# Far sets of a fused square-root and spectral kernel: turned tiles as moving operands only, the second one sent through memory

## The chip, the cores and the metric

The kernel runs on one core of one Trainium2 chip. The metric is device time in microseconds (us) of one launch. A core has five engines with their own instruction queues, each in order: TensorE (PE in the profile; its weight loads are PEld), VectorE (DVE), ScalarE (ACT), GpSimd (POOL) and SyncE (SP), which here only issues DMA transfers. ScalarE issues DMA transfers too. Matmuls write to PSUM, which has 8 banks; an instruction waits for others by semaphores.

## The reference

Two residual layers on x of shape (32, 32, 128, 128). The first normalises x by groups of channels and adds to x an approximate matrix square root of each of its 1024 matrices of 128 x 128, found by five coupled Newton-Schulz steps. The second normalises again and adds a spectral convolution.

```python
normA = sqrt(sum(A2 * A2, axis=(1, 2)))
Y, Z = A2 / normA, I
for _ in range(5):
    T = 0.5 * (3.0 * I - Z @ Y)
    Y, Z = Y @ T, T @ Z
x = x + Y * sqrt(normA)                      # of the group-normalised x
...
f = fftn(group_norm(x), axes=(2, 3)).real    # 32 x 32 corner modes, top and bottom
x = x + ifftn(einsum over channels(f, weights)).real
```

## The kernel before, in words

Four channels of one image make a set; there are 32 x 8 = 256 sets. A set is one generator, `newton` (line 447), which does a few products, yields, and goes on a round later. Up to eight sets are under way in eight lanes; a round goes through the lanes in order and lets each do one step. Line 88 keeps every instruction in program order on its engine, so the order of each queue is the order in which the rounds reach the steps. A new set starts every 23/8 rounds while far sets come (`FAR`, line 42). Far sets are those of images 1 to 18 (`is_far`, line 357): 144 sets. The others are near sets.

A set's work is a polynomial of m, the scaled matrix, put as products of four 128 x 128 matrices (`products`, line 345: four float32 matmuls, stationary operand first, into one PSUM bank). Each far set needs products with a transposed tile, and gets it without TensorE: VectorE turns each 32 x 32 block of a PSUM bank into the tile "turn" (0.7 us), and DMA transfers move the blocks to their places. `across` (line 420) does both: one transposition and four transfers on SP, one for each quarter of the partitions.

In this document step k is what a far set does after its k-th yield. Before the change:

- step 0: product of mb and m; the bank is turned and goes by four transfers into w; VectorE adds v to the same bank; GpSimd forms EYE_Q minus mb in place
- step 4: product of v and w; VectorE makes q
- step 6: product of q and m; ScalarE writes y, the first half of the tile "my"
- step 8: product of q and y; ScalarE writes the new m, the second half of "my"; then the bank is turned and goes by four transfers into mb, in runs of 32 numbers (128 bytes)
- step 10: GpSimd forms v = EYE_V minus m
- step 12: product of mb and m, in the profile "ps<-my,mb"; as step 0, with the transfers into w
- step 16: product of v and w; q
- step 18: four matmuls of double width, q times y and m side by side; ScalarE writes t and y4
- step 20: product of t and q; VectorE makes t
- step 22: product of t and y4, added to x

In the names of the profile the moving operand comes first: "ps<-my,mb" has mb stationary. Near sets use other steps, with transpositions on TensorE, and their own "my,mb", with mb copied by ScalarE.

Around the sets, in the same rounds, GpSimd and ScalarE scale the next sets' inputs (`staged`, line 374; x is m and b is mb of step 0); ScalarE issues the loads of coming inputs (`fetch`, line 366, and `prep`, line 222); SP stores each finished set into the scratch tensor mid (`settle`, line 496). `four` (line 312) hands out the buffers of each kind; `rooms` (lines 308 and 309) has two numbers for each: those that stay, and those there until the far sets are done.

Of the kernel before, what the change touches and what calls it, by code (L numbers as in the profile page):

```python
# [93 lines left out]
def conv_preact_kernel(  # L94
# [19 lines left out]
    nc.vector.tensor_scalar_mul(eye1[:, 0, :], ident, EYE)  # L114
    eye = eye1.to_broadcast([P, 4, P])
    eyes = []
    for n, f in (("v", EYE_V), ("q", EYE_Q), ("p", EYE_Q * TURNED)):
        e = const.tile([P, 1, P], F32, name=f"eye_{n}")
        nc.vector.tensor_scalar_mul(e[:, 0, :], ident, f)
        eyes.append(e.to_broadcast([P, 4, P]))  # L120
# [101 lines left out]
    def prep(bs, made):  # L222

        n = len(bs)
        nc_, ng = n * C, n * G
        first_b = bs[0]
        st = small.tile([P, ng, 6], F32, tag="a_st", name=f"a_st{first_b}", bufs=2)
        tiles = []
        parts = [(b, i) for b in bs for i in range(C // 4)]

        ahead = 3 if first_b else 8

        def load(k):
            b, i = parts[k]
            if first_b or i < 4:
                t = stp.tile([P, 2, 2 * P], F32, tag="xs", name=f"xs{b}_{i}")
            else:
                t = four("turn", True).rearrange("p (j c) x -> p j (c x)", j=2)
            src = xs_in[b, :, 2 * i : 2 * i + 2].rearrange("p g h c -> p g (h c)")
            kept(nc.scalar.dma_start(out=t, in_=src))  # L240
            tiles.append(t)

        for k in range(ahead):
            load(k)
        yield
        for k in range(len(parts)):
            for j in range(2):
                nc.vector.bn_stats(st[:, 2 * k + j, :], tiles[k][:, j, :])
            yield
            if k + ahead < len(parts):  # L250
                load(k + ahead)
        ms = small.tile([P, ng], F32, tag="a_ms", name=f"a_ms{first_b}")
        nm, d = yield from moments(st, ms, "a")
        yield from pause
        pq = bank()[:, 0, 0:nc_]
        nc.tensor.matmul(pq, avg_mean, d.rearrange("p g c -> p (g c)"), start=True, stop=True)
        if not first_b:
            warm(5)

        v = small.tile([P, nc_ + ng], F32, tag="a_v", name=f"a_v{first_b}")  # L260
        nc.vector.tensor_scalar_mul(v[:, 0:nc_], pq, -512 / (P * P))
        yield
        vg = small.tile([P, ng], F32, tag="a_vg", name=f"a_vg{first_b}")
        nc.vector.tensor_reduce(
            vg, v[:, 0:nc_].rearrange("p (g c) -> p g c", c=2), AX.X, ALU.add
        )
        nc.vector.tensor_scalar(v[:, nc_:], vg, 0.5, EPS, ALU.mult, ALU.add)
        yield
        s = small.tile([P, nc_ + ng], F32, tag="a_r_s", name=f"a_r_s{first_b}", bufs=2)
        yield from root(v, nc_ + ng, s)  # L270
        iv = small.tile([P, nc_ + ng], F32, tag="a_inv", name=f"a_inv{first_b}")
        nc.vector.reciprocal(iv, s)
        yield

        sc = small.tile([P, nc_], F32, tag="a_sc", name=f"a_sc{first_b}", bufs=2)
        nc.vector.tensor_scalar_mul(sc, iv[:, 0:nc_], MS / P)
        off = small.tile([P, ng, 2], F32, tag="a_off", name=f"a_off{first_b}", bufs=2)
        nc.vector.tensor_tensor(
            off,
            sc.rearrange("p (g c) -> p g c", c=2),  # L280
            nm[:, :, None].to_broadcast([P, ng, 2]),
            ALU.mult,
        )
        off = off.rearrange("p g c -> p (g c)")
        sn = small.tile([P, nc_], F32, tag="a_t_s", name=f"a_t_s{first_b}", bufs=3)
        for k, b in enumerate(bs):
            g, c = slice(k * G, k * G + G), slice(k * C, k * C + C)
            made[b] = (nm[:, g], sc[:, c], off[:, c], sn[:, c])
        yield
        nn = small.tile([P, ng, 2], F32, tag="a_d", name=f"a_n{first_b}")  # L290
        nc.vector.tensor_tensor(
            nn,
            s[:, 0:nc_].rearrange("p (g c) -> p g c", c=2),
            iv[:, nc_:, None].to_broadcast([P, ng, 2]),
            ALU.mult,
        )
        nn = nn.rearrange("p g c -> p (g c)")
        for far in sorted({is_far(b) for b in bs}):
            of = [k for k, b in enumerate(bs) if is_far(b) == far]
            c = slice(of[0] * C, of[-1] * C + C)  # L300
            f = EYE_Q * QS * TURNED**2 if far else EYE * QF
            nc.vector.tensor_scalar_mul(nn[:, c], nn[:, c], P * (1.5 / f) ** 2)
        yield
        yield from root(nn, nc_, sn)
        yield


    rooms = dict(b=(4, 4), xt=(10, 4), x=(3, 2), r=(4, 0), v=(3, 4), w=(3, 2), q=(4, 2))
    rooms.update(my=(4, 2), mb=(2, 3), t=(3, 2), y4=(2, 2), turn=(0, 4))
    turns = dict.fromkeys(rooms, 0)  # L310

    def four(tag, more):
# [22 lines left out]
    def blocks(t):  # L335


        return t.rearrange("p c x -> p (c x)").rearrange("p (a c j) -> p a c j", a=4, c=4)

    def minus(eye, m, t):  # L340

        nc.gpsimd.tensor_tensor(t, eye, m, ALU.subtract)
        return t
# [13 lines left out]
    def is_far(b):  # L357
        return 0 < b < FIRST
# [15 lines left out]
    def staged(b, g, nm, sc, off, sn):  # L374
# [10 lines left out]
        for j in range(4):  # L385
# [13 lines left out]
                on_scalar(m[:, j, :], xt[:, j, :], off, sc, c)  # L399
            on_scalar(mb[:, j, :], mb[:, j, :], off, sc, c)  # L400
            yield
        v = minus(eye_v, m, four("v", True)) if is_far(b) else None
        ready.append((xt, m, mb, v))
        yield

# [11 lines left out]
        yield from rest  # L417
        return q

    def across(ps, more, into):  # L420


        t = four("turn", more)
        nc.vector.transpose(blocks(t), ps.rearrange("p c (i b) -> p b c i", b=4))
        for a in range(4):
            src = t[32 * a : 32 * a + 32].rearrange("p c x -> p (c x)")
            kept(
                nc.sync.dma_start(out=into(a), in_=src.rearrange("p (b x) -> p b x", b=4))
            )

    def far_quartic(m, mb, v, more, f, eye_q):

        ps = products(mb, m)
        w = four("w", more)
        across(ps, more, lambda a: w.rearrange("p c x -> p (c x)")[:, P * a : P * a + P])
        nc.vector.scalar_tensor_tensor(v, ps, 1 / (9 * MS * f), v, ALU.mult, ALU.add)
        minus(eye_q, mb, mb)
        yield from rest
        yield from rest
        ps = products(v, blocks(w).rearrange("p a c j -> p c a j"))  # L440
        q = plus(ps, 9 / (39 * MS**2), mb, "q", more)
        yield from rest
        return q

# [2 lines left out]
    def newton(g, sn, xt, m, mb, v, far, more):  # L447


        qf = QS if far else QF  # L450
        if far:
            q = yield from far_quartic(m, mb, v, more, 1.0, eye_q)
        else:
            q = yield from near_quartic(m, mb, more)
        my = four("my", more)
        y = my[:, :, 0, :]
        nc.scalar.mul(y, products(q, m), 1 / (MS * qf))
        yield from rest
        m = my[:, :, 1, :]
        ps = products(q, y)  # L460
        nc.scalar.mul(m, ps, MS / qf)
        if far:
            mb = four("mb", more)
            across(ps, more, lambda a: mb[:, :, 32 * a : 32 * a + 32])
            yield from rest
            v = minus(eye_v, m, four("v", more))
            yield from rest
            qf, et, eye_t = QS * TURNED, EYE_Q * TURNED, eye_p
            q = yield from far_quartic(m, mb, v, more, TURNED, eye_p)
        else:  # L470
            yield from rest
            mb = taken(transposed(m), "mb", more)
            yield from rest
            et, eye_t = EYE, eye
            q = yield from near_quartic(m, mb, more)
        both = [bank().rearrange("p (j k) x -> p j k x", k=2) for _ in range(2)]
        for j in range(4):
            nc.tensor.matmul(both[j // 2][:, j % 2], q[:, j], my[:, j], start=True, stop=True)
        w, y = four("t", more), four("y4", more)
        for h in range(2):  # L480
            nc.scalar.mul(w[:, 2 * h : 2 * h + 2, :], both[h][:, :, 1, :], 1 / (MS * qf))
        for j in range(4):
            c = 4 * g + j
            nc.scalar.mul(y[:, j, :], both[j // 2][:, j % 2, 0, :], sn[:, c : c + 1])
        yield from rest
        t = plus(products(w, q), -0.5 * et / (1.5 * qf), eye_t, "t", more)
        yield from rest
        nc.vector.tensor_tensor(xt, products(t, y), xt, ALU.add)
        if not todo and lanes.count(None) == LANES - 1:
            warm(2)  # L490
        yield
# [707 lines left out]
```

## Time and profile before

| what | us |
|---|---|
| median of 3 runs | 3038.55 |
| lowest and highest | 3033.91, 3040.33 |
| the profiled execution, its own time | 3030.63 |
| its span, first to last instruction | 3028.5 |
| TensorE busy in the span | 2856.4 (94%) |
| VectorE busy | 2271.7 (75%) |
| GpSimd busy | 1995.5 (66%) |
| ScalarE busy | 1567.5 (52%) |

The durations below come from that one profiled execution. Matmul records overlap, so the starts of successive products tell TensorE's pace better than their durations. The chain of waits that ended last has 51% of the span on TensorE's matmuls, 17% on DMA transfers (4% w, 3% mb) and 5% on SP's queue. DMA moved 598.69 MB in 746612 packets, 403472 of them under 512 bytes.

### The profile page before, as it was taken

Reading aid. Unit: us, or ns where it says so; the run is one execution under the profiler, and the core shown is the slowest. Engines: PE = TensorE matmul, PEld = TensorE weight load, DVE = VectorE, ACT = ScalarE, POOL = GpSimd, SP = SyncE. Lnnn points to the kernel's source line nnn. Section 1 sums busy time; section 2 is a strip of 40 time slices with the busy share of each in tenths; the row PEclk is TensorE's granted clock in tenths of the full one; section 3 lists DMA queues with packets and bytes.
Section 4 is the critical chain, followed back from the end, with each engine's and each line's share of the span. In section 5 each row is a group of like instructions: output and inputs, shape, how many; then the busy total and the mean of one; then the engine's idle time right before and its main releaser. Section 6 shows DMA issues by size and latency. Waiting matters only on the chain.

```text
span 3028.5 us, 73234 instructions
## 1 busy us (share of the span) xinstructions
PE 2856.4 (94%) x26536; PEld 2636.7 (87%) x26536; DVE 2271.7 (75%) x4407; ACT 1567.5 (52%) x4043; POOL 1995.5 (66%) x2308
## 2 busy tenths in 40 slices
PE   7999999999999999999999999999989999999996
PEld 7999988989989898898899889888878899888884
DVE  7878787878878787878776645877886867777564
ACT  4555555555545555555544445555554544555452
POOL 4677766777767676777665534787777754678352
PEclk9999999999999999999999999999999999999997
DMA  5577777778676877777753566877867747666676
GB/s 178 153 202 173 197 181 178 185 181 205 165 199 166 210 167 204 171 204 174 199 137 99 160 208 206 269 245 252 274 231 253 246 123 214 214 220 216 179 223 247
DMA packets 746612, 598.69 MB, mean 198 GB/s; under 512 B 403472, under 2 KB 564240, under 8 KB 746256
## 3 DMA queue, kind: packets, MB, share of 16 engines
q1 hardware_dynamic: 632640, 385.56, 46.9%
q10 hardware_dynamic: 113616, 208.45, 21.7%
q8 instruction: 215, 3.52, 0.5%
q14 instruction: 141, 1.16, 0.1%
HBM read 326.93 MB, written 153.62 MB: 159 GB/s over the span
## 4 chain that ended last, share of the span: by engine, by line
PE 51%; DMA 17%; DVE 10%; POOL 9%; issue 5%; SPq 5%; ACT 2%; ACTq 1%; DVEq 0%; POOLq 0%
PE ps L88 51%; SPq L88 5%; DMA w<-turn 4%; DMA mb<-turn 3%; POOL yt L88 3%; DMA yt<-mid 2%; DMA mid<-xt 2%; POOL r L88 2%; POOL fold L88 2%; DVE turn L88 2%; POOL x L88 2%; DMA xs<-in_xs 1%; DVE v L88 1%; DVE yt L88 1%; DVE q L88 1%
## 5 line engine op out<-in xcount | busy, mean ns | idle before, releaser
L88 PE MATMUL ps<-my,q 128*128 128x128 f32 (+1 forms) x4096 | 749.7, 331 | 41.3 <-ACT my L88 21.0
L88 PEld LDWEIGHTS ps<-my,q 128*128 128x128 f32 x4096 | 623.6, 192 | 94.7 <-ACT my L88 23.6
L88 ACT ACTIVATE b<-b,a_off,a_sc 128x128 f32<-128x128 f32 x1024 | 467.9, 491 | 348.3 <-DMA b<-in_x 63.8
L88 PE MATMUL ps<-w,v 128*128 128x128 f32 x4096 | 550.4, 279 | 40.5 <-DVE w L88 15.9
L88 PEld LDWEIGHTS ps<-w,v 128*128 128x128 f32 x4096 | 499.7, 193 | 56.6 <-issue 23.4
L88 POOL TENSOR_TENSOR fold<-xt 128x256 f32<-128x256 f32 x512 | 363.7, 733 | 247.1 <-DVE xt L88 220.6
L88 ACT ACTIVATE my<-ps 128x512 f32<-128x512 f32 x512 | 305.7, 599 | 413.9 <-PE ps L88 386.3
L88 POOL TENSOR_TENSOR yt<-yt,d 128x512 f32<-128x512 f32 x244 | 306.8, 1282 | 221.5 <-ACT d L88 190.5
L88 DVE STREAM_TRANSPOSE turn<-ps 128x512 f32<-128x512 f32 x432 | 302.8, 705 | 178.4 <-ACT my L88 102.1
L88 POOL TENSOR_TENSOR v<-eye_v,x 128x512 f32<-128x512 f32 x144 | 183.6, 1275 | 262.7 <-ACT x L88 255.7
L88 POOL TENSOR_SCALAR x<-xt,a_nm,a_sc 128x128 f32<-128x128 f32 x736 | 324.9, 457 | 15.1 <-DVE a_sc L88 14.8
L88 ACT ACTIVATE t<-ps 128x256 f32<-128x256 f32 x512 | 186.9, 380 | 268.9 <-PE ps L88 255.6
L88 ACT ACTIVATE y<-ps,a_t_s 128x128 f32<-128x128 f32 x1024 | 291.4, 375 | 0.0
L88 PE MATMUL ps<-my,mb 128*128 128x128 f32 x2048 | 275.5, 278 | 10.7 <-DMA mb<-turn 4.8
L88 PE MATMUL ps<-x,b 128*128 128x128 f32 x2048 | 281.3, 280 | 1.1 <-ACT b L88 1.0
L88 PE MATMUL ps<-x,q 128*128 128x128 f32 x2048 | 277.5, 279 | 4.6 <-DVE q L88 2.6
L88 PE MATMUL ps<-q,t 128*128 128x128 f32 x2048 | 275.0, 278 | 6.8 <-ACT t L88 6.2
L88 PEld LDWEIGHTS ps<-my,mb 128*128 128x128 f32 x2048 | 259.8, 193 | 22.1 <-issue 9.1
L88 PE MATMUL ps<-y,t 128*128 128x128 f32 x2048 | 275.0, 278 | 0.3 <-DVE b_r L88 0.3
L88 POOL TENSOR_TENSOR mb<-eye_p,mb 128x512 f32<-128x512 f32 x144 | 184.0, 1278 | 133.1 <-PE ps L88 130.9
L88 PEld LDWEIGHTS ps<-x,q 128*128 128x128 f32 x2048 | 252.2, 194 | 15.9 <-issue 8.4
L88 PEld LDWEIGHTS ps<-q,t 128*128 128x128 f32 x2048 | 251.1, 193 | 9.2 <-ACT t L88 7.3
(132 smaller groups left out, 4776.4 us busy)
## 6 DMA issues: line engine op xcount, KB each, us to landing
w<-turn SPq DMA_DIRECT2D x1152, 64.0 KB
b<-in_x ACTq DMA_DIRECT2D x256, 256.0 KB
xt<-in_xt ACTq DMA_DIRECT2D x256, 256.0 KB
mid<-xt SPq DMA_DIRECT2D x256, 256.0 KB
yt<-mid SPq DMA_DIRECT2D x128, 512.0 KB
xs<-in_xs ACTq DMA_DIRECT2D x252, 256.0 KB
out<-yt SPq DMA_DIRECT2D x115, 512.0 KB
mb<-turn SPq DMA_DIRECT2D x576, 64.0 KB
```

The lines of the kernel that those rows point to most:

```text
L88: return self.tc.keep_in_program_order(issue(*args, **kw))
```

## The change

In far sets the other factor of each product becomes the stationary one, so that a turned tile is only ever the moving operand, which can be read in blocks. The second m's tile may then land in the block order in which w lands, in runs of 512 bytes. Its way is no longer four transfers from "turn" to mb in step 8, but one transfer from "turn" to a scratch tensor in memory in step 8, and one from there to mb in step 10. With this:

- in step 8 the transposition stands ahead of ScalarE's copy of the same bank
- v of the second quartic is formed in step 12 from mb as it landed, instead of in step 10 from m; VectorE adds to it in step 13 instead of step 12 (`later`)
- the subtraction in place is done on m, not on mb
- step 18 is two products of single width: q times mb, which ScalarE copies at once, and q times y
- b and mb have one more early buffer each
- constants are scaled for the tile that is used

```diff
-    for n, f in (("v", EYE_V), ("q", EYE_Q), ("p", EYE_Q * TURNED)):
+    for n, f in (("v", EYE_V), ("q", EYE_Q), ("p", EYE_V * TURNED)):
...
-    rooms = dict(b=(4, 4), xt=(10, 4), x=(3, 2), r=(4, 0), v=(3, 4), w=(3, 2), q=(4, 2))
-    rooms.update(my=(4, 2), mb=(2, 3), t=(3, 2), y4=(2, 2), turn=(0, 4))
+    rooms = dict(b=(4, 5), xt=(10, 4), x=(3, 2), r=(4, 0), v=(3, 4), w=(3, 2), q=(4, 2))
+    rooms.update(my=(4, 2), mb=(2, 4), t=(3, 2), y4=(2, 2), turn=(0, 4))
...
+    def turned(ps, more):
         t = four("turn", more)
         nc.vector.transpose(blocks(t), ps.rearrange("p c (i b) -> p b c i", b=4))
+        return t
+
+    def by_rows(t):
+        return blocks(t).rearrange("p a c j -> p c a j")
+
+    def far_quartic(m, mb, v, f, later, more):
+        ps = products(m, mb)
+        t, w = turned(ps, more), four("w", more)
         for a in range(4):
             src = t[32 * a : 32 * a + 32].rearrange("p c x -> p (c x)")
...
-        nc.vector.scalar_tensor_tensor(v, ps, 1 / (9 * MS * f), v, ALU.mult, ALU.add)
-        minus(eye_q, mb, mb)
-        yield from rest
+        minus(eye_q, m, m)
+        if later:
+            yield
+        nc.vector.scalar_tensor_tensor(v, ps, 1 / (9 * MS), v, ALU.mult, ALU.add)
+        if not later:
+            yield
+        yield
         yield from rest
-        ps = products(v, blocks(w).rearrange("p a c j -> p c a j"))
-        q = plus(ps, 9 / (39 * MS**2), mb, "q", more)
+        q = plus(products(v, by_rows(w)), 9 / (39 * MS**2 * f**2), m, "q", more)
...
-        ps = products(q, y)
-        nc.scalar.mul(m, ps, MS / qf)
+        ps = products(y, q) if far else products(q, y)
         if far:
+            t = turned(ps, more)
+            held = dram.tile([P, 512], F32, name="turn", tag="turn", bufs=4)
+            kept(nc.sync.dma_start(out=held, in_=t.rearrange("p c x -> p (c x)")))
+            nc.scalar.mul(m, ps, MS / qf)
+            yield from rest
             mb = four("mb", more)
-            across(ps, more, lambda a: mb[:, :, 32 * a : 32 * a + 32])
+            src = held.rearrange("(a i) (b x) -> (i b) a x", a=4, b=4)
+            into = mb.rearrange("p c x -> p (c x)").rearrange("p (a x) -> p a x", a=4)
+            kept(nc.sync.dma_start(out=into, in_=src))
             yield from rest
-            v = minus(eye_v, m, four("v", more))
-            yield from rest
-            qf, et, eye_t = QS * TURNED, EYE_Q * TURNED, eye_p
-            q = yield from far_quartic(m, mb, v, more, TURNED, eye_p)
+            v = four("v", more)
+            form = "p c (a j) -> p c a j"
+            minus(eye_p.rearrange(form, a=4), by_rows(mb), v.rearrange(form, a=4))
+            q = yield from far_quartic(m, by_rows(mb), v, TURNED, True, more)
+            w, y4 = four("t", more), four("y4", more)
+            nc.scalar.mul(w, products(q, by_rows(mb)), 1 / (MS * qf * TURNED))
+            ps = products(q, y)
+            for j in range(4):
+                c = 4 * g + j
+                nc.scalar.mul(y4[:, j, :], ps[:, j, :], sn[:, c : c + 1])
```

`rest` is two yields, so the steps keep their numbers.

More of the change, by code (lines that the diff above doesn't have):

```diff
@@ L300, in prep @@
             c = slice(of[0] * C, of[-1] * C + C)
-            f = EYE_Q * QS * TURNED**2 if far else EYE * QF
+            f = EYE_Q * QS if far else EYE * QF
             nc.vector.tensor_scalar_mul(nn[:, c], nn[:, c], P * (1.5 / f) ** 2)
@@ L401, in staged @@
             yield
-        v = minus(eye_v, m, four("v", True)) if is_far(b) else None
+        v = minus(eye_v, mb, four("v", True)) if is_far(b) else None
         ready.append((xt, m, mb, v))
@@ L418, in near_quartic @@
         return q
-    def across(ps, more, into):
+    def turned(ps, more):
         t = four("turn", more)
         nc.vector.transpose(blocks(t), ps.rearrange("p c (i b) -> p b c i", b=4))
+        return t
[4 more added lines that the diff above has]
+        t, w = turned(ps, more), four("w", more)
         for a in range(4):
@@ L427, in across @@
             kept(
-                nc.sync.dma_start(out=into(a), in_=src.rearrange("p (b x) -> p b x", b=4))
-            )
[L431 to L435, printed above, removed]
-        nc.vector.scalar_tensor_tensor(v, ps, 1 / (9 * MS * f), v, ALU.mult, ALU.add)
-        minus(eye_q, mb, mb)
+                nc.sync.dma_start(
+                    out=w.rearrange("p c x -> p (c x)")[:, P * a : P * a + P],
+                    in_=src.rearrange("p (b x) -> p b x", b=4),
+                )
+            )
+        minus(eye_q, m, m)
[5 more added lines that the diff above has]
+        yield
         yield from rest
-        yield from rest
-        ps = products(v, blocks(w).rearrange("p a c j -> p c a j"))
-        q = plus(ps, 9 / (39 * MS**2), mb, "q", more)
+        q = plus(products(v, by_rows(w)), 9 / (39 * MS**2 * f**2), m, "q", more)
         yield from rest
@@ L447, in newton @@
     def newton(g, sn, xt, m, mb, v, far, more):
-        qf = QS if far else QF
+        qf, et, eye_t = (QS, EYE_Q, eye_q) if far else (QF, EYE, eye)
         if far:
-            q = yield from far_quartic(m, mb, v, more, 1.0, eye_q)
+            q = yield from far_quartic(m, mb, v, 1.0, False, more)
         else:
@@ L456, in newton @@
         y = my[:, :, 0, :]
-        nc.scalar.mul(y, products(q, m), 1 / (MS * qf))
+        nc.scalar.mul(y, products(q, mb if far else m), 1 / (MS * qf))
         yield from rest
         m = my[:, :, 1, :]
-        ps = products(q, y)
-        nc.scalar.mul(m, ps, MS / qf)
+        ps = products(y, q) if far else products(q, y)
         if far:
+            t = turned(ps, more)
[3 more added lines that the diff above has]
+            yield from rest
             mb = four("mb", more)
-            across(ps, more, lambda a: mb[:, :, 32 * a : 32 * a + 32])
+            src = held.rearrange("(a i) (b x) -> (i b) a x", a=4, b=4)
+            into = mb.rearrange("p c x -> p (c x)").rearrange("p (a x) -> p a x", a=4)
+            kept(nc.sync.dma_start(out=into, in_=src))
             yield from rest
-            v = minus(eye_v, m, four("v", more))
-            yield from rest
-            qf, et, eye_t = QS * TURNED, EYE_Q * TURNED, eye_p
-            q = yield from far_quartic(m, mb, v, more, TURNED, eye_p)
+            v = four("v", more)
[8 more added lines that the diff above has]
+                nc.scalar.mul(y4[:, j, :], ps[:, j, :], sn[:, c : c + 1])
         else:
+            nc.scalar.mul(m, ps, MS / qf)
             yield from rest
@@ L473, in newton @@
             yield from rest
-            et, eye_t = EYE, eye
             q = yield from near_quartic(m, mb, more)
[L476 to L484, printed above, removed]
+            both = [bank().rearrange("p (j k) x -> p j k x", k=2) for _ in range(2)]
+            for j in range(4):
+                nc.tensor.matmul(both[j // 2][:, j % 2], q[:, j], my[:, j], start=True, stop=True)
+            w, y4 = four("t", more), four("y4", more)
+            for h in range(2):
+                nc.scalar.mul(w[:, 2 * h : 2 * h + 2, :], both[h][:, :, 1, :], 1 / (MS * qf))
+            for j in range(4):
+                c = 4 * g + j
+                nc.scalar.mul(y4[:, j, :], both[j // 2][:, j % 2, 0, :], sn[:, c : c + 1])
         yield from rest
@@ L487, in newton @@
         yield from rest
-        nc.vector.tensor_tensor(xt, products(t, y), xt, ALU.add)
+        ps = products(y4, t) if far else products(t, y4)
+        nc.vector.tensor_tensor(xt, ps, xt, ALU.add)
         if not todo and lanes.count(None) == LANES - 1:
```

## The prediction

> **What bounds the kernel now.** I read the shares by engine first, then the stage by windows. The transfers of turned tiles, which only far sets have, run from 89.4 to 1570.2 us (below), so the stretch from 90 to 1575 us counts. The windows view gives it one line (length, then busy us and instructions of PE, PEld, DVE, ACT and POOL, granted clock, DMA share, GB/s):
>
> ```profile
> 90.00:1575.00 1485.00, 1416.70 (x11589) 1333.61 (x11588) 1204.92 (x2390) 800.37 (x2127) 1058.15 (x1170) 0.99 0.74 184
> ```
>
> The reader is to see that TensorE is idle for only 1485.0 − 1416.7 = 68 us here, 0.47 us a set: the stage's 1163 double-width matmul records, eight a set, make 145 sets of 10.2 us (the 144 far ones and a near neighbour). That is all a better hidden transfer can win. VectorE is busy for 81%, so it often runs behind. The waits view of the stage says what the idle time hung on (total, times, longest), first for PE, then for DVE:
>
> ```profile
> PE ps L88 <- ACT my L88: 17.2, 8, 3.7
> PE ps L88 <- DMA mb<-turn: 11.9, 10, 3.5
> PE ps L88 <- DVE q L88: 10.0, 11, 1.3
> ```
>
> ```profile
> DVE turn L88 <- ACT my L88: 102.1, 91, 4.5
> DVE turn L88 <- PE ps L88: 65.9, 91, 1.4
> ```
>
> So the trip of the second m costs TensorE 12 us today, and VectorE loses 102 us because the transposition of step 8 stands behind ScalarE's copy of the same bank. Next the issuing engine: the view of tile "turn" has issue times in ns (min/median/max), the timeline of SP shows them in a row, and the timeline of PE the same stretch:
>
> ```profile
> L88 SPq DMA_DIRECT2D w<-turn x1152: 542/602/1930, 89.4 to 1570.2; - x192
> L88 SPq DMA_DIRECT2D mb<-turn x576: 609/632/1985, 110.2 to 1558.2; - x192
> ```
>
> ```profile
> 743.91 2.83 SPq L88 DMA_DIRECT2D mb<-turn  x4
> 746.79 0.62 SPq L88 DMA_DIRECT2D mid<-xt  x1
> 747.51 5.13 SPq L88 DMA_DIRECT2D w<-turn  x8
> 752.75 2.69 SPq L88 DMA_DIRECT2D mb<-turn  x4
> 755.48 0.62 SPq L88 DMA_DIRECT2D mid<-xt  x1
> 756.20 6.05 SPq L88 DMA_DIRECT2D w<-turn  x8
> ```
>
> ```profile
> 743.10 1.89 PE L88 MATMUL ps<-my,q 128*128 128x256 f32 x8
> 744.83 1.05 PE L88 MATMUL ps<-my,mb 128*128 128x128 f32 x8
> ...
> 753.25 1.05 PE L88 MATMUL ps<-my,mb 128*128 128x128 f32 x8
> ...
> 758.03 1.06 PE L88 MATMUL ps<-w,v 128*128 128x128 f32 x8
> 758.92 1.06 PE L88 MATMUL ps<-q,t 128*128 128x128 f32 x8
> 759.82 1.06 PE L88 MATMUL ps<-my,q 128*128 128x128 f32 x8
> 760.71 1.06 PE L88 MATMUL ps<-my,mb 128*128 128x128 f32 x8
> ```
>
> SP issues almost without a gap: 8 × 0.60 + 4 × 0.63 + 0.62 = 8.0 of 10.2 us. A product of four starts every 0.89 us (758.03, 758.92, 759.82), the double-width one takes 1.73 (743.10 to 744.83). "my,mb" is step 12, the reader of the second m's turned tile; it comes every 7 to 16 us.
>
> **What the Trainium skill says.** "PSUM — Partial Sum Buffer", Terms: two engines may not touch one PSUM bank at once, reads included. The 102.1 us above are this rule at work: whichever of transposition and copy comes first in program order, the other waits. "DMA: Bandwidth & Descriptors", Rules for kernel authors: a DMA that reads what an earlier one wrote must wait, on the issuing engine, for the earlier one's semaphore; the trace of before has no such pair in this stage, the new one will. Same page, Specifications: full rate needs runs of 512 bytes. The trace's packets agree: 128-byte ones take 13 ns (median), 512-byte ones 27, 2 KB ones 84. "TensorE: Matmul & The Clock Gate", HAM oscillation: idle gaps of some 3.4 us halve the clock. After a gap of 2.48 us at 1003.6 us the next three products took 1.26, 1.71 and 1.44 us instead of 0.89, so long gaps cost more than themselves.
>
> **The change part by part.** *Products.* The double-width product of step 18 becomes two. By starts: 2 × 0.89 − 1.73 = +0.05 us, +8 us over 144 sets. By busy time it would be (2 × 275.9 − 491.6) / 2048 × 1152 = +34 us; matmuls overlap, so I take 8 and keep 34 for the range. Exchanging stationary and moving operand costs nothing: the rows with a turned tile moving ("w,v", 279 ns) and a plain one (278) are equal.
>
> *ScalarE.* Two copies of 380 ns become one of 599: −23 us in all, hidden, since ScalarE is busy for 54% of the stage. In step 8 the order turns round: the transposition goes first, ScalarE's "my" waits for it with the fetches and copies behind. VectorE can win up to its 102 us, ScalarE can lose as much; for PE's sum I take 0 and keep ±15 us, about the 17.2 that PE now waits for "my".
>
> *GpSimd.* Four subtractions of 1.28 us before and after. One now reads blocks of 32; "fold" with short runs has 733 ns for half the elements, 15% over, so 0 to 0.2 us, hidden at 71% busy. But it moves from step 10 to 12 and waits for the landing, with the other lanes' folds and norms behind it, and its reader on VectorE stands one round later (step 13). At about 3.5 us a round that holds; what is lost there I put at 0 to 20 us, in the range.
>
> *DMA work.* 2048 packets of 128 bytes (13.8 ns mean) are 28 us of engine time a set; 128 of 2 KB (89) and 512 of 512 bytes (34) are 29. No gain. *SP's issues.* Twelve become ten: −4 × 0.63 + 2 × 0.63 = −1.26 us a set.
>
> *The trip itself.* Before, all four issues stand in step 8 and the data is wanted in step 12. Issue end to use was 746.74 to 753.25, 6.5 us; landing takes about 2, so there was slack. Now step 8 only stores. The load is issued in step 10, and on SP everything issued in between is ahead of it. The order of SP's instructions in the changed kernel, built and read, is for nearly every set: store, eight transfers into w, load. So the load cannot leave before the last transposition ahead of it is done, and its four issues: 2.5 us for one w, 5 for two. Landing: the loads of 256 KB on ScalarE's queue took 3.1 us from issue to last packet (median of 436 in the stage, 2.5 to 4.5 for 9 of 10); I take 3.1 + 0.1.
>
> Put into the lines above: with a store in place of the four, the eight transfers that follow run 745.2 to 750.3 (their transpositions were ready at 744.02 and 746.64), load 750.3, landed 753.5, wanted 753.25. A draw. For the next set the step-12 product of 753.25 must itself be turned (0.89 + 0.15 + 0.70: 755.0 if VectorE is free; in fact it was ready at 759.22, behind a chain of small ones), its w ends at 759.0, the load lands at 762.2 and is wanted at 760.71: 1.5 us late, 4.4 with VectorE's real delay.
>
> The same for all cases: PE's order in the changed kernel repeats every eight sets. From a step-8 product to the step-12 product that needs its tile are 14, 15, 14, 12, 15, 14, 12, 14 products at 0.97 us (10.2 less 0.47 idle, by ten). In between, w is turned from the products numbered (2,5), (3,5), (2,5), (2,5), (1,3), (3,6), (4,6), (1,3); each is ready 0.8 us after its end, takes 2.5 us of SP, the second not before the first is out; then 3.2 us. Slack: 1.3, 1.7, 1.3, −0.7, 3.6, 0.3, −2.2, 2.6 us, less VectorE's delay. Half of the transpositions begin within 0.5 us of their product, a quarter over 2.6 late. With 0.3 throughout, PE stalls 1.0 + 2.5 = 3.5 us in eight sets, 0.44 each; with 2.6 in half of the cases, 1.09. A stall lets VectorE catch up, so I take 0.65 × 144 = 94 us, between 38 (landing in 2.5 us) and 157. The stalls swallow some idle time: the 11.9 us on "mb" and a quarter of the other 56, together 26.
>
> Sum: +94 − 26 + 8 = +76 us on the profiled 3030.63 us (span 3028.5 and 2.1 around it), +2.5%; on the median of 3038.55, which lies 0.26% above that run, 3115 us.
>
> **Rivals.** *The relief wins.* SP at 8.0 of 10.2 us is nearly full, and w leaves a median of 3.9 us after its transposition. With 1.26 us less, and 102 us of VectorE's waiting gone, every landing comes earlier; if VectorE then runs within 0.3 us and the load lands in 2.5, the deficits fall to some 0.3 us a set and mostly fall into gaps that exist. Worth 45% of the 68 us: −30 + 8 = −22, 3016 us. It decides once a load leaves SP 3 us before its product in all but one case of eight. For it speaks the full SP line, against it that the load must queue behind the same eight transfers. *Both cancel:* 3038 us. *Another wait in its place:* landing in time, but the later reader of v on VectorE holds one of eight PSUM banks a round longer, and GpSimd waits in line; 20 us + 8 − 12: 3055 us. *The change doesn't do what it says:* the transfers are as told in the built order; no weight.
>
> **How the numbers follow.** Load late 0.58, relief 0.25, cancelled 0.09, other wait 0.08. Below 0.2% (6 us) a change can't be told from none. Slower 0.66, same 0.09, faster 0.25. The likeliest has 3065 to 3200 (38 − 26 + 8 to 157 with half of the bounds of the others). To hold 8 in 10 the range reaches into the relief: 3010 to 3200.
>
> **What would show it.** Right: PE waits for "DMA mb" rise from 11.9 us to 80 or more, in a few of every eight sets, 2 us and over; SP's load begins right after eight w; DVE's wait for "my" is gone and ACT waits for "turn". Wrong: loads leave SP 4 us ahead of step 12, PE's idle time in the stage falls below 50 us.

## The result, and the profile after

The changed kernel takes 3281.78 us (median of 4 runs, 3270.61 to 3284.75) against 3036.41 for the kernel before (now 4 runs too): a ratio of 1.08, 95% interval 1.077 to 1.083. Slower, as forecast, but by 245 us where 76 were forecast, and outside the range. The profiled run of the changed kernel has a span of 3277.4 us, 248.9 more than before.

First where the time lies. The windows view of the changed kernel, far sets and the rest (length, then busy us and instructions of PE, PEld, DVE, ACT and POOL, granted clock, DMA share, GB/s):

```profile
90.00:1815.00 1725.00, 1501.54 (x12702) 1443.58 (x12702) 1186.58 (x2387) 791.64 (x1985) 1059.76 (x1169) 0.94 0.62 180
1815.00:3277.00 1462.00, 1369.91 (x14429) 1239.82 (x14426) 1004.89 (x1851) 727.73 (x1816) 897.46 (x1075) 0.97 0.65 212
```

The far stage grew from 1485 to 1725 us, 240 of the 249. VectorE, ScalarE and GpSimd do the same work as before within 2%. TensorE differs twice: it is idle for 1725.0 − 1501.5 = 223.5 us instead of 68.3, and it is *busy* for 85 us more, at a granted clock of 0.94 instead of 0.99. DMA got lighter on average (share 0.62 instead of 0.74), so its mean load is not it; how long the single load takes is told below.

Next what the engines waited for in the stage (total, times, longest): PE, then POOL, ACT and DVE.

```profile
PE ps L88 <- DMA mb<-turn: 208.4, 82, 5.9
```

```profile
POOL v L88 <- DMA mb<-turn: 299.7, 79, 8.0
```

```profile
ACT my L88 <- DVE turn L88: 386.3, 122, 9.0
```

```profile
DVE turn L88 <- PE ps L88: 365.3, 190, 6.7
```

One wait carries nearly all of TensorE's idle time: the load of the second m's tile, late 82 times in 144 sets, by 2.5 us on average. GpSimd stands for the same load. VectorE no longer stands behind ScalarE's copy (102.1 us before, no such line now); ScalarE stands behind VectorE instead, and VectorE behind TensorE. These look like followers of the one late transfer, round the loop.

Then one loop, in the timelines of SP and of PE in the same stretch (start, length, idle before and its releaser in brackets):

```profile
999.68 6.81 SPq L88 DMA_DIRECT2D w<-turn  x8
1006.60 0.57 SPq L88 DMA_DIRECT2D mb<-turn  x1
1007.27 0.59 SPq L88 DMA_DIRECT2D mid<-xt  x1
1009.23 0.32 SPq L88 DMA_DIRECT2D turn<-turn  x1
1013.76 5.88 SPq L88 DMA_DIRECT2D w<-turn  x8
1019.75 0.53 SPq L88 DMA_DIRECT2D mb<-turn  x1
```

```profile
1005.90 1.06 PE L88 MATMUL ps<-q,my 128*128 128x128 f32 x8
1010.93 2.05 PE L88 MATMUL ps<-mb,my 128*128 128x128 f32 x8 [3.98 <-DMA mb<-turn]
1012.77 1.92 PE L88 MATMUL ps<-b,q 128*128 128x128 f32 x8
1014.48 1.89 PE L88 MATMUL ps<-b,x 128*128 128x128 f32 x8
1016.18 1.08 PE L88 MATMUL ps<-mb,q 128*128 128x128 f32 x8
...
1026.57 1.06 PE L88 MATMUL ps<-mb,my 128*128 128x128 f32 x8
```

The load "mb<-turn" is issued 0.1 us after the eighth transfer into w, 4.3 us ahead of its product. And after the gap of 3.98 us the next three products start 1.84, 1.71 and 1.70 us apart instead of 0.89: the lowered clock costs another 2.6 us. The product "b,x", whose turned tile goes out ahead of the *next* load, moves with them: it starts 3.55 us after step 12's, where it would be 1.78 at full clock. But the reader of that next load stands behind the same slow products on TensorE. It starts at 1026.57, 6.8 us after its load was issued (1019.75), and does not wait. The chain of waits ahead of the late product takes the way over SP (the number after the time is the length):

```profile
1000.28 2.08 DMA w<-turn
1002.36 0.70 DVE turn L88
...
1004.32 1.52 SPq L88
...
1006.60 4.20 DMA mb<-turn
```

### The profile page after: what moved, and what is told of

Its sections match the earlier page's. It is cut to its first block, busy times and chain, and to the rows that moved or that the text cites. A ratio compares the mean times of both kernels' runs of the same rounds, so it can differ in the third digit from the quotient of the medians.

```text
span 3277.4 us, 74759 instructions
## 1 busy us (share of the span) xinstructions
PE 2946.2 (90%) x27688; PEld 2751.9 (84%) x27688; DVE 2259.1 (69%) x4407; ACT 1559.7 (48%) x3899; POOL 1999.0 (61%) x2308
## 4 chain that ended last, share of the span: by engine, by line
PE 52%; DMA 19%; DVE 10%; POOL 7%; SPq 6%; issue 5%; ACT 2%; ACTq 0%; DVEq 0%; POOLq 0%
PE ps L88 52%; DMA mb<-turn 10%; SPq L88 6%; DMA w<-turn 3%; POOL yt L88 2%; DVE turn L88 2%; POOL r L88 1%; POOL x L88 1%; DVE q L88 1%; DVE v L88 1%; DVE yt L88 1%; DMA yt<-mid 1%; POOL fold L88 1%; DMA xs<-in_xs 1%; DMA mid<-xt 1%
## 5 line engine op out<-in xcount | busy, mean ns | idle before, releaser
L88 PE MATMUL ps<-w,v 128*128 128x128 f32 x4096 | 548.4, 280 | 17.2 <-DVE w L88 15.0
L88 PE MATMUL ps<-my,q 128*128 128x128 f32 (+1 forms) x2944 | 475.2, 310 | 15.5 <-DVE q L88 10.9
L88 PEld LDWEIGHTS ps<-my,q 128*128 128x128 f32 x2944 | 414.8, 192 | 42.3 <-issue 11.7
L88 PE MATMUL ps<-mb,my 128*128 128x128 f32 x1152 | 189.8, 317 | 215.1 <-DMA mb<-turn 208.4
L88 POOL TENSOR_TENSOR v<-eye_p,mb 128x512 f32<-128x512 f32 x144 | 183.1, 1272 | 299.7 <-DMA mb<-turn 299.7
L88 PEld LDWEIGHTS ps<-mb,my 128*128 128x128 f32 x1152 | 166.4, 222 | 229.6 <-issue 167.0
L88 POOL TENSOR_TENSOR v<-eye_v,b 128x512 f32<-128x512 f32 x144 | 183.8, 1276 | 163.5 <-ACT b L88 163.4
L88 POOL TENSOR_TENSOR x<-eye_q,x 128x512 f32<-128x512 f32 x144 | 183.9, 1277 | 152.6 <-PE ps L88 152.3
L88 ACT ACTIVATE t<-ps 128x256 f32<-128x256 f32 (+1 forms) x368 | 170.9, 466 | 209.0 <-PE ps L88 196.3
L88 DVE SCALAR_TENSOR_TENSOR q<-ps,eye 128x512 f32<-128x512 f32 x224 | 153.6, 686 | 135.0 <-PE ps L88 131.1
L88 DVE BATCH_NORM_STATS2 a_st<-xs 128x6 f32<-128x256 f32 x504 | 185.5, 411 | 55.3 <-DMA xs<-in_xs 55.3
```

The lines of the kernel that those rows point to most:

```text
L88: return self.tc.keep_in_program_order(issue(*args, **kw))
```

## The experiments

**The load on another queue.** Only the issuing engine of the load is changed:

```diff
-            kept(nc.sync.dma_start(out=into, in_=src))
+            kept(nc.scalar.dma_start(out=into, in_=src))
```

> The changed kernel, with the load of step 10 issued by ScalarE instead of SP. Theory A (the load is late because it stands behind eight transfers into w on SP): on ScalarE it leaves soon after step 8's copy and lands 3 to 4 us later, ahead of step 12; PE's wait for mb falls from 208 us to under 40 and the time to 3020 to 3070 us. Rival B (two trips through memory take too long whatever the queue): the wait stays over 100 us and the time over 3150 us. Rival C (the rest of the change, such as roles of the operands or the moved v, costs the time): over 3150 us with little wait for mb.

Measured: 3068.83 us, ratio to the kernel before 1.0116 (1.0084 to 1.0149). PE's line in the waits view:

```profile
PE ps L88 <- DMA mb<-turn: 63.0, 40, 4.4
```

Same bytes, same trip through memory, and six sevenths of the loss are gone. The wait for mb stayed above the 40 us expected: in the 40 sets that still wait, the product starts a median of 4.6 us after the load is issued, where 3 to 4 were expected.

**No memory trip.** In step 8 the turned tile goes straight to mb in four transfers of 512-byte runs; all else is as in the changed kernel:

```diff
-            held = dram.tile([P, 512], F32, name="turn", tag="turn", bufs=4)
-            kept(nc.sync.dma_start(out=held, in_=t.rearrange("p c x -> p (c x)")))
-            nc.scalar.mul(m, ps, MS / qf)
-            yield from rest
             mb = four("mb", more)
-            src = held.rearrange("(a i) (b x) -> (i b) a x", a=4, b=4)
-            into = mb.rearrange("p c x -> p (c x)").rearrange("p (a x) -> p a x", a=4)
-            kept(nc.sync.dma_start(out=into, in_=src))
+            for a in range(4):
+                src = t[32 * a : 32 * a + 32].rearrange("p c x -> p (c x)")
+                into = mb.rearrange("p c x -> p (c x)")[:, P * a : P * a + P]
+                kept(nc.sync.dma_start(out=into, in_=src.rearrange("p (b x) -> p b x", b=4)))
+            nc.scalar.mul(m, ps, MS / qf)
+            yield from rest
```

> The changed kernel without the trip through memory: in step 8 four transfers go straight from the turned tile to mb, in runs of 512 bytes; all else stays changed. Theory A: 3020 to 3060 us, since step 12 has its tile as early as in the kernel before. Rival C: over 3150 us. Rival B says nothing against 3020 to 3060.

Measured: 3023.41 us, ratio 0.9957 (0.9945 to 0.9969). So the rest of the change, operand roles, two single products, the moved subtraction and addition, costs nothing together; the version is 0.4% faster than the kernel before. All of the 245 us is in how the second tile travels.

**The same four transfers, late.** The version above with the four issues moved to step 10, behind the eight into w, and no memory involved:

```diff
+            nc.scalar.mul(m, ps, MS / qf)
+            yield from rest
             mb = four("mb", more)
             for a in range(4):
...
-            nc.scalar.mul(m, ps, MS / qf)
-            yield from rest
```

> The version with four direct transfers and no memory trip, with the four issued in step 10 instead of step 8, so that they stand behind the same eight transfers into w as the changed kernel's load. Theory A (the place in SP's queue is the cause): no memory is involved, yet the time is as bad as the changed kernel's 3282 us or worse, since four issues and a landing take some 4.6 us against the load's 3.2: 3300 to 3500 us. Rival B (the trip through memory is what is slow): under 3100 us.

Measured: 3368.63 us, ratio 1.111 (1.1071 to 1.1148), with this line for PE:

```profile
PE ps L88 <- DMA mb<-turn: 268.6, 88, 5.8
```

So a loss of this size needs no trip through memory, and the place in SP's queue is enough by itself: with the same transfers the time is 12 us under the kernel before from step 8 and 335 us over it from step 10. That the turned tile is held until step 10 is not what costs: VectorE waits for a free "turn" for 31.8 us in all, each time on the transfers into w. Nor is step 10 too late as such: the load on ScalarE left in step 10 too, and most of the loss was gone.

**The load one step earlier, on SP.**

```diff
             nc.scalar.mul(m, ps, MS / qf)
-            yield from rest
+            yield
             mb = four("mb", more)
...
             kept(nc.sync.dma_start(out=into, in_=src))
+            yield
             yield from rest
```

> The changed kernel with the load issued in step 9 instead of step 10, still by SP. It then stands ahead of about two thirds of the groups of w that it followed, but right behind the store, so SP waits for the store to land (some 3 us). Theory A: half to three quarters of the loss goes, 3080 to 3160 us, the rest being SP's waits for the store. Rival B: over 3200 us.

Measured: 3181.62 us, ratio 1.0488 (1.0445 to 1.0531), so 40% of the loss goes, less than expected. SP's own waits, over the whole span, say why:

```profile
SPq L88 <- DMA turn<-turn: 192.9, 70, 6.1
```

Now the load stands right behind its store, and SP, in order, holds all transfers into w for 193 us until stores have landed. PE still waits 134.2 us for mb. Neither place tried on SP is good for the second of two dependent transfers: early it blocks the queue, late it is blocked.

**The load on ScalarE and one step earlier.** Both edits above.

> The changed kernel with the load issued by ScalarE and in step 9. If the 63 us of waiting for mb that are left with ScalarE's load in step 10 come from the load's late place alone: under 30 us of waiting, 3030 to 3055 us. If ScalarE now stands for the store's landing with its copies behind it, as SP did: 3070 us or more, with the waiting moved to other copies of ScalarE.

Measured: 3083.85 us, ratio 1.0158 (1.0119 to 1.0197), no better than on ScalarE in step 10. PE's waits in order:

```profile
PE ps L88 <- ACT my L88: 34.1, 27, 3.7
PE ps L88 <- DVE w L88: 17.7, 12, 3.1
PE ps L88 <- DMA mb<-turn: 17.0, 14, 1.9
```

The wait for mb fell from 63.0 to 17.0 us, as the first case expected, and the time is that of the second: TensorE's wait for ScalarE's "my" rose from 16.4 to 34.1 us, and ScalarE now stands for the store's landing ahead of other copies (17.2 us ahead of z, 16.8 ahead of b). A wait for a landing, put into another in-order queue, moves here to what stands behind it.

**Useless work in the gap.** In every far set two matmuls of 512 columns, read by nobody, stand ahead of step 12's product in the changed kernel:

```diff
+            warm(2)
             q = yield from far_quartic(m, by_rows(mb), v, TURNED, True, more)
```

> The changed kernel with two idle matmuls of 512 columns (some 1.7 us of useless work, into a bank of their own) ahead of the product of step 12 in every far set. They run while TensorE would stand. Theory D (the gaps also lower the clock, and slow products delay the next transpositions and so the next load): shorter gaps keep the clock up, and in spite of 144 x 1.7 = 245 us of useless work the time is no higher than the changed kernel's 3282 us. Rival (the waits cost only themselves): 62 of 144 sets have no wait and pay in full, over 100 us, so 3350 to 3420 us.

Measured: 3269.46 us, ratio 1.0783 (1.0758 to 1.0808); the interval overlaps the changed kernel's. Its windows line for the far stage, the lines of waits of PE and POOL, and a gap of the timeline:

```profile
90.00:1800.00 1710.00, 1649.19 (x13150) 1458.68 (x13150) 1181.05 (x2367) 785.91 (x1968) 1052.15 (x1160) 0.99 0.62 180
```

```profile
PE ps L88 <- DMA mb<-turn: 57.5, 36, 4.0
```

```profile
POOL v L88 <- DMA mb<-turn: 278.6, 82, 6.1
```

```profile
1007.40 1.88 PE L88 MATMUL ps<-tab,ident 128*128 128x512 f32 x4
1010.50 1.13 PE L88 MATMUL ps<-mb,my 128*128 128x128 f32 x8 [1.21 <-DMA mb<-turn]
1011.46 1.06 PE L88 MATMUL ps<-b,q 128*128 128x128 f32 x8
1012.36 1.06 PE L88 MATMUL ps<-b,x 128*128 128x128 f32 x8
1013.25 1.06 PE L88 MATMUL ps<-mb,q 128*128 128x128 f32 x8
```

The clock is back at 0.99, and the products after the load start 0.96 and 0.90 us apart: the gaps did lower the clock. Some 245 us of useless matmuls cost nothing net, since they stand where TensorE waited or where its products ran slowly. The loads themselves are hardly less late: GpSimd, which runs no filler, waits for them for 278.6 us, against 299.7 in the changed kernel. So theory D's forecast of the time came true, but only its first half, the clock, is shown. What slow products do to the next load this run does not separate, and TensorE is now busy for 96% of the stage (1649 of 1710 us), so neither does it show that TensorE's work has no part in the stage's length.

**The pair of products alone.** The kernel before, with step 18 of far sets as in the changed one:

```diff
+        if far:
+            w, y4 = four("t", more), four("y4", more)
+            nc.scalar.mul(w, products(q, m), 1 / (MS * qf))
+            ps = products(q, y)
```

> The kernel before, with step 18 of far sets as two single-width products and one copy of t, and nothing else. By starts of products +8 us (0.3%), by busy time +34 us (1.1%). If it is over 1.1%, the pair of products is dearer than either reading.

Measured: 3049.22 us, ratio 1.0051 (1.0026 to 1.0075), so +14 us (3035.16 for the kernel before in these rounds), between both readings and nearer to that by starts.

**The order of transposition and copy.** Twice: put into the kernel before alone (transposition first), and taken out of the version without the memory trip (copy first).

```diff
-        nc.scalar.mul(m, ps, MS / qf)
         if far:
             mb = four("mb", more)
             across(ps, more, lambda a: mb[:, :, 32 * a : 32 * a + 32])
-            yield from rest
+        nc.scalar.mul(m, ps, MS / qf)
+        if far:
+            yield from rest
```

> The kernel before, with the transposition of step 8 ahead of ScalarE's copy, and nothing else. If the order alone is worth it: 3020 to 3030 us, and VectorE's 102 us of waiting for my are gone. My sum of the prediction: within 15 us of 3038. If ScalarE's waiting costs as much as VectorE wins: no change.

> The version with four transfers and no memory trip, with ScalarE's copy of m put back ahead of the transposition in step 8. If its 12 us over the kernel before come from the order of transposition and copy: back to 3035 to 3050 us. If they come from elsewhere (operand roles, runs of 512 bytes, buffers): 3015 to 3030 us.

Measured: in the kernel before 3037.98 us, ratio 1.0021 (1.0009 to 1.0032); copy first in the other version 3028.71 us, ratio 0.9989 (0.9978 to 1.0), against 0.9957 with the transposition first. VectorE's 102 us of waiting did go in the first, and ScalarE waited 249.4 us for "turn" instead. In microseconds the second run lies in the range set for "elsewhere", but the kernel before was faster in these rounds as well (3031.59 against 3035.16); by the ratios three quarters of the small gain went with the order. Putting the transposition first is worth +0.2% in one kernel and −0.3% in the other: no rule follows from it.

**The addition back in step 12.** The version without the memory trip, with `later` False.

```diff
-            q = yield from far_quartic(m, by_rows(mb), v, TURNED, True, more)
+            q = yield from far_quartic(m, by_rows(mb), v, TURNED, False, more)
```

> The version with four transfers and no memory trip, with VectorE's addition to v back in step 12 instead of 13. If VectorE then waits for GpSimd's subtraction in every set: 3040 to 3070 us. If GpSimd is quick enough: within 6 us of 3023.

Measured: 3017.23 us, ratio 0.996 (0.9944 to 0.9976). VectorE waits for GpSimd's v only 38 times, 59.0 us in all, and the time shows none of it: the later addition buys nothing here. This version and the one with the addition in step 13 are both 0.4% faster than the kernel before, and can't be told apart.

## Why the prediction was right and wrong

The direction held, and so did the mechanism: the load queues on SP behind the transfers into w. In 126 of the 144 sets the instruction ahead of it on SP is such a transfer, and nine loads of ten are issued 0.1 us after the end of what stands ahead. The two places of the same transfers (12 us under the kernel before in step 8, 335 over it in step 10) show the queue to be the cause. The rival "relief" was wrong from its own point of decision: 82 of 144 loads, not one in eight, held TensorE up. The other wait (addition in step 13) was worth nothing in the version without the memory trip.

The sum failed in its terms. Against the four of the prediction, for the far stage:

| term | forecast, us | measured, us |
|---|---|---|
| waiting for the load | 94 | 208.4 |
| idle time swallowed | −26 | −53 |
| two products for one | +8 | about +14 |
| lower clock | 0 | about +71 |
| sum | 76 | 240 |

The swallowed time is 11.9 for mb and 56.4 − (223.5 − 208.4) = 41 of the rest. The pair is measured by itself at 0.5% of the whole. The clock's share is what is left of the 85 us of added busy time, so the sum comes out by construction. There is a second way to it: the starts of successive matmuls that lie over 1.3 times their usual distance apart add some 76 us more than in the kernel before with the pair of products.

Two terms failed. The larger is the stall, in the step "takes 2.5 us of SP, the second not before the first is out; then 3.2 us", from which 0.65 us a set followed: it was 208.4 / 144 = 1.45, above both ends (0.44 and 1.09). For each of the 82 sets that wait, the traces of TensorE, VectorE and SP give the way from the last turned product ahead of the load to the load's reader (mean us):

| part of the way | forecast | measured |
|---|---|---|
| end of the product to the tile turned | 0.8, and VectorE's delay | 1.13 |
| from there to the issue of the load on SP | 2.5, more behind another tile | 3.85 |
| issue of the load to its product | 3.2 | 4.22 |
| sum | 6.5 and more | 9.20 |
| TensorE's other products meanwhile | 0.97 each | 6.66 for 7.0, 0.95 each |

The difference, 9.20 − 6.66 = 2.54 us, is the wait of a set that waits. TensorE's pace was right, and VectorE's delay small (mean 0.43 us, median 0.04), as was assumed for a stage with stalls. SP and the landing were not: with every landing held to 3.2 us and all else as it was, the 82 waits would come to an estimated 136 us, and with SP held to 2.5 us as well to 60. On SP, 0.84 of the 3.85 us pass before the tile's first transfer is issued. Why the load took 3.8 us (median) where ScalarE's loads of the same size had taken 3.1 before stays open.

The other failed term is the lower clock, which the prediction put at nothing, though it had quoted the slowdown after a gap of 2.48 us ("long gaps cost more than themselves"); it came to some 71 us. It is a loss beside the stalls, and nothing shows that it feeds them. The slow products after a gap delay a later reader as much as the tile turned ahead of its load, or more. And the waits show no build-up: they follow the cycle of eight sets. Counted by a set's place in it, from the first far set on, they sum to 53, 9, 53, 55, 0, 28, 1 and 9 us.

Two smaller judgements stood: a turned tile as the moving operand costs nothing that the version without the memory trip would show, and ScalarE's and VectorE's change of places is near zero.

## What to carry to other kernels

Before splitting a transfer into two dependent ones, read what the in-order queue has between the two places: the second can't leave before everything ahead of it has been released, and the slack is counted from there, not from the step in which the data becomes ready. Where the slack is a few us, take the queue's time and the landing as they are in that place: here 1.35 and 1.0 us too little made most of the 208 us of waiting (by the estimate above). Price a stall of TensorE with the clock it costs as well. A wait for a landing belongs on a queue with nothing urgent behind it, and moving it only helps if there is such a queue.

## What the runs showed of the hardware that was not expected

The time that SP takes to issue a transfer does not follow its size. From the view of tile "turn" of the changed kernel (ns, min/median/max):

```profile
L88 SPq DMA_DIRECT2D w<-turn x1152: 542/602/2099, 90.2 to 1813.1; - x192
L88 SPq DMA_DIRECT2D turn<-turn x144: 319/326/4084, 111.0 to 1796.7; - x144
L88 SPq DMA_DIRECT2D mb<-turn x144: 371/538/2937, 114.8 to 1802.7; - x144
```

A store of 256 KB in one piece is issued in 0.33 us, one transfer of 64 KB between partitions in 0.60; the prediction had taken 0.63 for the store and for the load.

The clock fell after shorter gaps than the 3.4 us that the prediction quotes. In the changed kernel, the first three products from step 12's on took 0.97, 0.99 and 0.87 us (medians) after the 30 gaps under 2 us, 0.99, 1.64 and 0.89 after the 12 of 2 to 2.5 us, and 1.84, 1.71 and 1.41 after the 21 over 3.5 us. And some 245 us of useless matmuls in the gaps kept the stage's clock at 0.99 instead of 0.94 and left the time at 3269 us against 3282.
